# A conditioned transformer layer on one core: queue order of transfers, times of the norm's steps, and the place of one subtraction

## The chip, the cores and the metric

The kernel runs on one core of a Trainium2 chip. The core has five engines with a program each: TensorE (PE in the profile; its weight loads are PEld), VectorE (DVE), ScalarE (ACT), GpSimd (POOL) and SyncE (SP, which here issues nearly all DMA transfers). Every engine works through its own instructions in order and waits on semaphores for the others. The metric is the device time of one launch in microseconds (us); lower is better.

## The reference

One layer of a transformer with adaptive layer norm, over 8 sequences of 1024 tokens with 512 features, all in fp32:

```python
mod = silu(condition) @ Wada + bada
sh_a, sc_a, gt_a, sh_m, sc_m, gt_m = split(mod, 6)
xm = layernorm(x, g1, be1) * (1 + sc_a) + sh_a
x = x + gt_a * attention(xm, Wqkv, Wproj, bproj)   # causal, 16 heads of 32
xm = layernorm(x, g2, be2) * (1 + sc_m) + sh_m
x = x + gt_m * (gelu(xm @ W1 + b1) @ W2 + b2)      # 512 -> 2048 -> 512
```

## The kernel before

**Blocks.** The tokens are cut into 16 blocks n of 512 tokens; blocks 2b and 2b+1 are the halves of sequence b. A block goes through: load of x (`load_x`, tile hat), norm a, q, k and v, attention with its own keys and those of the earlier half, projection with the residual (`load_xr`, tile xr), norm m, four up steps with gelu (tiles hT), four down parts, and the store. The blocks are interleaved by a table, `plan` (L273 to L317): while the attention of block w runs, the projection and the feed-forward of block w-1 and the norm and q, k, v of the next blocks are put between its matmuls, so that TensorE has products to do while softmax work goes on elsewhere.

**Products.** Each 512-wide linear product is done by seven half-size products instead of eight (the Strassen-Winograd form, `strassen`, L959). Sums of weight quarters are made once and kept in DRAM (kept_qkv_S, kept_proj_S, kept_up_S, kept_down_S); sums of activations (t_a, t_m, t) are made per block. For the down product the halves of the gelu's output hT are the operands: B12 stands for the second token half, and the product needs B12 minus B11. `combine` (L1294, its operation at L1299) makes this difference in place on DVE at the start of down part 0. All linear matmuls go through `matmul` (L233) into one of three PSUM banks; results leave through `copy_out` (L214 or L217) and `combine_out` (L222).

**Attention.** For the row maxima, scores go to sc (L1692), DVE adds the mask (L1706) and reduces (L1709); the maxima are split in bf16 terms (mcols, L1728 to L1731), transposed by TensorE (L1747) and copied (mrow, L1753). Transposed scores st start with minus the maximum (L1773) and add the products (L1785); ACT takes the exponent into pT (L1798), POOL masks it (affine select, L1803) and adds the chunks of keys up (L1911), TensorE multiplies with v (po, L1826), and `finish` (L1836) sums over the keys by a product with ones (L1847). ACT inverts the sum (rec) and POOL or DVE scales.

**Weights and transfers.** Weight pieces of 256 KB come through a ring of nine tiles w. `fetch` (L380) issues a piece as soon as a ring tile is released; a piece is issued at L390, a kept sum at L392. SP issues in order, so a transfer that waits holds back those behind it. The other transfers are: loads of x for a norm (L432 and L438), loads of xr (L1443), stores of the output (L1276), gate rows, and the way by which a block is transposed for most norms. That way is `turn_rows` (L758): DVE turns squares of 32 by 32, four puts (L776, 256 KB each) write them to DRAM, and one get (L782, 1 MB) reads all channels back into xm; then DVE (L841) or ACT (L847) applies scale and shift to a channel group at a time.

**The planner.** The order on every engine is fixed while the program is built. The kernel keeps a clock for each engine (`now`), and for each piece of data the time when it will be written or left (`note`, `due`). Work that isn't due waits in lists: `jobs` for DVE (statistics, turns), `pool_jobs` for residual adds, `excursions` for ACT steps of a norm (root and apply, set off at fixed places of the attention by `run_excursions`), `transfers` for puts, gets and stores. Between matmuls `step_aside` (L1552) and `work` put out what has come due. `either` (L179) gives an elementwise operation to DVE (L187) or POOL (L190), whichever its clocks say ends first. `run_transfers` (L628 on) lets the earliest transfer out when its time has come and keeps 700 ns between two; the loads of x and xr don't pass through it and are issued where the plan has them. The planned time of a get is 7000 ns behind the last put, and its data count as there 5000 ns later; xr rows count as there 10000 ns after the load, and 700 ns more for each further tile. `finish` begins with `run_jobs(True)`, which puts out all waiting DVE jobs whether due or not. `settle` (L1258) multiplies a down result by its gate and adds it to xr, through `either`.

Of the kernel before, what the change touches and what calls it, by code (L numbers as in the profile page):

```python
# [22 lines left out]
def kernel(  # L23
# [261 lines left out]
    for w in range(1, NB):  # L285
        n = w - 1
        m = mlp_steps(n)
        even = blocks[n][1] == 0
        rows_a = [("rows", blocks[n][0], "a")] if even else []
        rows_m = [("rows", blocks[n][0], "m")] if even else []  # L290
        at = [("at", w + 2)] if w + 2 < NB else []
        ups = m[:1] + ([("load_xa", w + 2)] if w + 2 < NB else []) + m[1:3]
        ups += ([("norm_a", w + 2)] if w + 2 < NB else []) + m[3:4] + at
        head = rows_a + [("load_xr", n)]
        if w == 1:
            steps = head + [("k", w + 1), ("proj", n), ("mt", n), ("q", w + 1)]
# [12 lines left out]
        if w == NB - 1:  # L309
            plan[w] += late + downs[:2]  # L310
            downs = downs[2:]
# [113 lines left out]

    def load_x(n):
        b, h = blocks[n]
        rows = row_tile(f"hat_{n}")
        if is_turned(f"a{n}"):
            for a in range(P // SQ):  # L430
                r0 = h * TB + a * P
                nc.sync.dma_start(  # L432
                    rows[a * SQ : (a + 1) * SQ, :, :],
                    x[b, r0 : r0 + P, :].rearrange("(t r) d -> r t d", r=SQ),
                )
        else:
            for t in range(NTT):
                nc.sync.dma_start(rows[:, t, :], x[b, h * TB + t * P : h * TB + (t + 1) * P, :])  # L438
        return [rows[:, t, :] for t in range(NTT)]

    x_pre = {0: load_x(0)}
    ada = {}
# [184 lines left out]

    transfers = []  # L628
# [23 lines left out]
    def excursion(job, reads, first=False):  # L652
        if alone[0]:
            job()
        else:
            excursions.insert(0 if first else len(excursions), (job, reads))
# [16 lines left out]
    def normalize(tiles, key, sources):  # L673
# [7 lines left out]

        def statistics(t):
            st = small.tile([P, nc.vector.BN_STATS_DIM], F32, tag="st", name=f"st_{key}_{t}")
            nc.vector.bn_stats(st, tiles[t])
            nc.vector.bn_aggr(mv[:, t, :], st)
# [62 lines left out]
    def turn_first():  # L748
# [7 lines left out]
        first_turned.append(st)  # L756

    def turn_rows(key, tiles, xm):  # L758

# [3 lines left out]
        def turn(t):  # L763
            nc.vector.transpose(
                squares[:, :, ts(t, SQ)], tiles[t].rearrange("p (k r) -> p k r", r=SQ)
            )
            note("DVE", 700, [("hat", key, t)], [])
            if t == NTT - 1:
                ready = now["DVE"] + SYNC
                for a in range(P // SQ):  # L770
                    transfers.append((ready, lambda a=a: put(a)))

        def put(a):
            if a == P // SQ - 1:
                transfers.append((queue_free[0] + 7000, get))
            nc.sync.dma_start(  # L776
                there[:, ts(a, P)].rearrange("(k r) n -> r k n", r=SQ),
                squares[a * SQ : (a + 1) * SQ, :, :],
            )

        def get():
            nc.sync.dma_start(xm, there.rearrange("(c p) n -> p c n", p=P))  # L782
            written["spread", key] = queue_free[0] + 5000

        written["spread", key] = NEVER
        for t in range(NTT):
            add_job(lambda t=t: turn(t), [("hat", key, t)], key)

    def modulated(key, gain, shift, b, guards):
# [27 lines left out]
        if rows_turned:  # L817
            turn_rows(key, got, xm)
            yield [("spread", key)], []
        for c in range(NC):  # L820
            if rows_turned:
                if c:
                    yield [("spread", key)], []
                from_ps, held = xm[:, c, :], ("spread", key)
            elif turned is None:
# [271 lines left out]

    residual, stored, unstored = {}, {}, []
    y_count, y_keys = [0], {}

    def y_key(kind, new=False):
# [4 lines left out]
        return y_keys[kind]  # L1106
    LANDING = 10000

# [27 lines left out]
    def project_half(n):  # L1136
# [5 lines left out]
        for t in range(NTT):  # L1142
            xt_job = lambda t=t: add_to(
                residual[n][:, t, :], gate_rows["gba"], [("row", "gba")], [("xr", n, t)]
            )
            pool_jobs.append((xt_job, [("xr", n, t)]))

        def put(f, t, bank, ps, other, reads, last):
# [7 lines left out]
            else:  # L1156
                combine_out(y, bank, ps, other, reads, [ky], last=last)
                add_to(y, gate, [("row", "ga")], [ky], ALU.mult)
            add_to(residual[n][:, half(t, 2), c], y, [ky], [("xr", n, 2 * t), ("xr", n, 2 * t + 1)])

        def done():
            run_pool_jobs(True)
            normalize([residual[n][:, t, :] for t in range(NTT)], f"m{n}", [("xr", n, t) for t in range(NTT)])
# [5 lines left out]
    def project_out(n):  # L1169
# [4 lines left out]
        for t, xt in enumerate(tiles):  # L1174
            xt_job = lambda t=t, xt=xt: add_to(xt, gate_rows["gba"], [("row", "gba")], [("xr", n, t)])
            pool_jobs.append((xt_job, [("xr", n, t)]))
# [47 lines left out]
    def up(step):  # L1224
        _, n, q = step

        def gelu():
            for i in range(NC):
# [4 lines left out]
                k = q // 2 + 1  # L1233
                note_act(590, "gelu", [("h", n, q)], [(n, f"B{k}1"), (n, f"B{k}2"), ("g", n, q)])

        def finished():
# [4 lines left out]
        if (n, q) == (0, 0):  # L1241
            yield ["prepared up"], []
        written["g", n, q] = NEVER
        hT = act.tile([P, NC, TB], F32, tag="hT", name=f"hT_{n}_{q}", bufs=NQ)
        hTs[n, q] = hT
# [20 lines left out]
    def store(n, t):  # L1266
# [3 lines left out]
        stored[n + 1] = max(stored.get(n + 1, 0.0), ready)  # L1270
        unstored.append(n)

        def move():
            unstored.remove(n)
            for i in (2 * t, 2 * t + 1):
                nc.sync.dma_start(rows[i], residual[n][:, i, :])  # L1276

        transfers.append((ready + 1000, move))

# [4 lines left out]
    def down(n, part):  # L1284
# [133 lines left out]
    def perform(step):  # L1418
# [9 lines left out]
        elif kind == "load_xa":  # L1428
            x_pre[step[1]] = load_x(step[1])
            written["x", f"a{step[1]}"] = now["PE"] + 6000  # L1430
        elif kind == "load_xr":
# [7 lines left out]
            else:  # L1439
                xr = xrp.tile([P, NTT, D], F32, tag="xr", name=f"xr_{n}")  # L1440
            residual[n] = xr
            for t, rows in enumerate(row_tiles_of(x[b, h * TB : (h + 1) * TB, :], n)):
                nc.sync.dma_start(xr[:, t, :], rows)  # L1443
                landed = max(now["PE"], stored.get(n - 1, 0.0)) + LANDING + 700 * t
                written["xr", n, t] = landed
        elif kind == "norm_a":
# [72 lines left out]
    def work():  # L1519
# [11 lines left out]
        run_jobs()  # L1531
        run_pool_jobs()
        run_transfers()
        run_preparation()
# [17 lines left out]
    def step_aside(reads, writes):  # L1552
# [14 lines left out]
        run_jobs()  # L1567
        run_pool_jobs()
        run_transfers()
        run_preparation()  # L1570
# [525 lines left out]
```

## Time and profile before

| what | value |
|---|---|
| median of 3 runs | 3471.28 us (3470.78 to 3471.49) |
| the profiled execution | 3470.92 us |
| its span (first to last instruction) | 3469.2 us |
| granted TensorE clock, mean | 1.000 |
| DMA traffic | 489.91 MB, mean 141 GB/s |
| moved per issue, weights | 256 KB |
| LDWEIGHTS and matmul records | 55,442 each |

The page gives the busy time of each engine as a sum and a share of the span. The list of waits gives, for an engine and a line, what it waited for: the total in us, how often, and the longest. A timeline row gives the start, the duration from first to last of the grouped instructions, the engine, the line, the operation with output and input tiles, and in brackets the idle time of the engine just before, with what ended it. A window row gives for a stretch each engine's busy time with its count of instructions, then the granted clock of TensorE, the share of busy DMA engines and GB/s. Groups give count, then busy us and mean ns, then the idle time before them. The slices of the page show TensorE at 0.9 or more in all but the first of 40:

```profile
PE   8999999999999999999999999999999999999999
```

### The profile page before, as it was taken

How to read it: one execution, taken by the hardware profiler on the slowest of the kernel's cores; microseconds unless marked ns; L12 is line 12 of the kernel's file. 1: busy time of each engine (PE TensorE's matmuls, PEld its weight loads, DVE VectorE, ACT ScalarE, POOL GpSimd, SP SyncE). 2: the span in 40 equal slices, each digit the busy share in tenths (PEclk: the TensorE clock that was granted, in tenths of full speed). 3: DMA queues.
4: the chain of work that ended last, by engine and by line, in shares of the span. 5: the costliest groups of instructions: out<-in, count | busy, mean ns of one | idle time of the engine just before them, and what ended most of it. 6: DMA issues, size and time to landing. Idle time of an engine off the chain costs nothing.

```text
span 3469.2 us, 122474 instructions
## 1 busy us (share of the span) xinstructions
PE 3423.4 (99%) x55442; PEld 1778.0 (51%) x55442; DVE 2055.4 (59%) x2262; ACT 1301.4 (38%) x1444; POOL 1944.2 (56%) x2101
## 2 busy tenths in 40 slices
PE   8999999999999999999999999999999999999999
PEld 5544554555545554455554555454554545544555
DVE  6765666646565465664756547575466745656364
ACT  2345244343343433434333353443524334242421
POOL 3766757656267471774626755277553774446530
PEclk9999999999999999999999999999999999999999
DMA  6833434345544454444544445444464454633444
GB/s 226 277 127 87 120 108 138 109 117 159 156 141 134 127 152 146 138 136 128 167 135 144 136 132 175 127 140 135 133 187 121 129 150 121 187 115 88 120 143 136
DMA packets 378508, 489.91 MB, mean 141 GB/s; under 512 B 27284, under 2 KB 234444, under 8 KB 377988
## 3 DMA queue, kind: packets, MB, share of 16 engines
q1 hardware_dynamic: 377792, 481.79, 47.1%
q8 instruction: 437, 7.16, 0.9%
q14 instruction: 83, 0.68, 0.1%
q10 hardware_dynamic: 196, 0.28, 0.0%
HBM read 428.44 MB, written 53.53 MB: 139 GB/s over the span
## 4 chain that ended last, share of the span: by engine, by line
PE 89%; DVE 4%; DMA 4%; ACT 1%; issue 1%; POOL 1%; SPq 0%; DVEq 0%; ACTq 0%; POOLq 0%
PE bank L233 62%; PE sc L1692 8%; PE po L1826 7%; PE st L1785 7%; PE st L1773 3%; DVE mx L1709 2%; DMA w<-kept_proj_S 2%; PE bank L1847 2%; DMA w<-in_L_cond_Wproj_dram 1%; DVE sc L1706 1%; ACT pT L1798 1%; DMA xm_m<-turned_m 1%; PE bank L1747 0%; DVE hT L1299 0%; DMA xr<-in_x_dram 0%
## 5 line engine op out<-in xcount | busy, mean ns | idle before, releaser
L1911 POOL TENSOR_TENSOR pT<-pT,pT 128x256 f32<-128x256 f32 (+3 forms) x1254 | 1213.5, 1003 | 143.1 <-ACT pT L1798 112.3
L1798 ACT ACTIVATE pT<-st 128x2048 f32<-128x2048 f32 x288 | 541.1, 1879 | 1075.2 <-PE st L1785 989.3
L233 PE MATMUL bank<-w,hT 128*32 128x256 f32 x14336 | 814.1, 380 | 0.0
L1709 DVE TENSOR_REDUCE mx<-sc 128x4 f32<-128x2048 f32 (+3 forms) x384 | 665.7, 1754 | 215.3 <-PE sc L1692 209.2
L233 PEld LDWEIGHTS bank<-w,hT 128*32 128x32 f32 x14336 | 454.5, 110 | 357.6 <-issue 74.7
L233 PE MATMUL bank<-xm_m,w 128*32 128x256 f32 x8192 | 500.7, 381 | 4.6 <-DVE xm_m L841 4.5
L1803 POOL TENSOR_SCALAR_AFFINE_SELECT pT<-pT 128x512 f32<-128x512 f32 x256 | 177.1, 710 | 436.8 <-ACT pT L1798 431.5
L233 PE MATMUL bank<-t_m,w 128*32 128x256 f32 x6144 | 384.2, 381 | 0.1
L233 PEld LDWEIGHTS bank<-xm_m,w 128*32 128x32 f32 x8192 | 257.2, 110 | 228.7 <-issue 65.1
L1692 PE MATMUL sc<-kT,qT 32*128 32x512 f32 (+3 forms) x3072 | 329.3, 520 | 2.9 <-DVE mx L1709 1.8
L1706 DVE TENSOR_TENSOR sc<-sc,mask 128x1024 f32<-128x1024 f32 (+1 forms) x160 | 162.8, 1017 | 242.9 <-PE sc L1692 167.2
L1826 PE MATMUL po<-pT,v 128*32 128x512 f32 (+3 forms) x3072 | 304.9, 491 | 0.0
L1785 PE MATMUL st<-qT,kT 32*128 32x512 f32 (+3 forms) x3072 | 300.1, 486 | 0.0
L233 PEld LDWEIGHTS bank<-t_m,w 128*32 128x32 f32 x6144 | 190.2, 110 | 178.4 <-issue 51.7
L233 PE MATMUL bank<-xm_a,w 128*32 128x256 f32 x3968 | 239.3, 380 | 2.4 <-ACT xm_a L847 1.1
L190 POOL TENSOR_TENSOR qT<-top,rec 128x512 f32<-128x512 f32 x60 | 78.5, 1309 | 276.1 <-ACT rec L1865 276.1
L222 DVE TENSOR_TENSOR hT<-bank,u_u 128x512 f32<-128x512 f32 x192 | 130.0, 686 | 153.2 <-PE bank L233 150.7
L1692 PEld LDWEIGHTS sc<-kT,qT 32*128 32x128 f32 x3072 | 129.7, 184 | 161.5 <-issue 54.7
L233 PE MATMUL bank<-w,qT 128*32 128x256 f32 (+1 forms) x2944 | 191.6, 399 | 3.2 <-DMA w<-in_L_cond_Wproj_dram 3.2
L233 PE MATMUL bank<-t_a,w 128*32 128x256 f32 x2944 | 181.7, 380 | 0.0
L233 PEld LDWEIGHTS bank<-xm_a,w 128*32 128x32 f32 x3968 | 127.7, 110 | 97.4 <-issue 13.9
L1230 ACT ACTIVATE hT<-hT,cols 128x512 f32<-128x512 f32 x256 | 164.2, 711 | 27.2 <-DVE hT L222 26.5
(240 smaller groups left out, 3418.2 us busy)
## 6 DMA issues: line engine op xcount, KB each, us to landing
w<-in_L_cond_W_dram SPq DMA_DIRECT2D x384, 256.0 KB
w<-kept_up_S SPq DMA_DIRECT2D x256, 256.0 KB
w<-kept_down_S SPq DMA_DIRECT2D x256, 256.0 KB
w<-kept_qkv_S SPq DMA_DIRECT2D x180, 256.0 KB
w<-in_L_cond_Wqkv_dram SPq DMA_DIRECT2D x147, 256.0 KB
hat<-in_x_dram SPq DMA_DIRECT2D x64, 256.0 KB
xr<-in_x_dram SPq DMA_DIRECT2D x64, 256.0 KB
out_dram<-xr SPq DMA_DIRECT2D x64, 256.0 KB
```

The lines of the kernel that those rows point to most:

```text
L222: nc.vector.tensor_tensor(out, src, other, op)
L233: nc.tensor.matmul(ps[r], columns, rhs, start=start, stop=stop, skip_group_check=True)
L1230: nc.scalar.activation(hT[:, i, :], hT[:, i, :], AF.Gelu, bias=cols[:, O_B1 + f : O_B1 + f + 1])
L1692: nc.tensor.matmul(sc[:, j, c0 : c0 + w], qTs[n][r, gg, ts(qt, P)], keys_of(n, kh)[r, gg, :w], start=True, stop=True, skip_group_check=True,)
L1706: nc.vector.tensor_tensor(place, place, shape_of.to_broadcast(place.shape), ALU.add)
L1709: nc.vector.tensor_reduce(maxima[n, gg][:, kh, qt, :], sc[:, :, c0 : c0 + w], axis=AX.X, op=ALU.max)
L1773: nc.tensor.matmul(st[:, j, c0 : c0 + w], minus_ones[r, :], row[r, TB - w :], start=(c0 == 0), stop=False, skip_group_check=True,)
L1785: nc.tensor.matmul(st[:, j, c0 : c0 + w], kT[r, gg, ts(k % NTT, P)], qT[r, gg, TB - w :], start=False, stop=True, skip_group_check=True,)
L1798: nc.scalar.activation(pT[:, :, :used], st[:, :, :used], AF.Exp, scale=scale)
L1803: nc.gpsimd.affine_select(diagonal, diagonal, pattern=[[0, HPG], [1, P]], compare_op=ALU.is_ge, fill=0.0, base=0, channel_multiplier=-1,)
L1826: nc.tensor.matmul(po[r, TB - w :], v[:, k % NTT, g * P + j * hd : g * P + (j + 1) * hd], pT[:, j, c0 : c0 + w], start=(k == 0), stop=last ...
L1911: nc.gpsimd.tensor_tensor(into, into, pT[:, j, c0 : c0 + w], ALU.add)
```

## The change

1. Transfers get a rank: puts and gets first, then loads of x and xr, then stores. `run_transfers` takes the lowest rank among those that are due and keeps 1700 ns between two instead of 700. The loads of x and xr now pass through this queue too; a consumer calls `arrived`, which puts the queue out where the load hasn't been issued yet. A store of two tiles becomes two transfers. The planned landing of an xr row becomes 6000 ns after its issue.
2. The get becomes four, one for each channel group of 256 KB, planned 5500 ns behind the last put and counted as there 3000 ns after the issue; scale and shift of a group wait for its own part.
3. Root and apply of a norm are put out by `run_ready` as soon as they are due, if ACT holds the table for the exponent. The gelus, which enter the same list with `first`, keep their set places.
4. The difference B12 minus B11 becomes a DVE job added behind the gelu of up steps 0 and 1; down part 0 waits for it ahead of its second product.
5. From the second sequence on, the gate rows of the attention are loaded one window earlier.

```diff
-        rows_a = [("rows", blocks[n][0], "a")] if even else []
+        rows_a = [("rows", blocks[n][0], "a")] if n == 0 else []
...
-        plan[w] = steps + rows_m + ups[:i]
+        rows_a = [("rows", blocks[w][0], "a")] if not even else []
+        plan[w] = steps + rows_m + rows_a + ups[:i]
...
+        for to, from_x in pairs:
+            later(lambda to=to, from_x=from_x: nc.sync.dma_start(to, from_x))
...
+    PATH, LOAD, STORE = range(3)
+    SPACE = 1700
...
-            i = min(range(len(transfers)), key=lambda i: transfers[i][0])
-            if not everything and max(queue_free[0], transfers[i][0]) > now["PE"]:
+            due_now = [i for i, (ready, *_) in enumerate(transfers) if ready <= now["PE"]]
+            if everything:
+                i = min(range(len(transfers)), key=lambda i: transfers[i][0])
+            elif queue_free[0] > now["PE"] or not due_now:
                 return
-            ready, transfer = transfers.pop(i)
-            queue_free[0] = max(queue_free[0], now["PE"], ready) + 700
+            else:
+                i = min(due_now, key=lambda i: transfers[i][1::-1])
+            ready, _, transfer = transfers.pop(i)
+            queue_free[0] = max(queue_free[0], now["PE"], ready) + SPACE
...
+    def run_ready():
+        while excursions and excursions[0][2]:
+            if table[0] != "exp" or max(now["ACT"], due(excursions[0][1])) > now["PE"]:
+                return
+            excursions.pop(0)[0]()
...
-                transfers.append((queue_free[0] + 7000, get))
+                for c in range(NC):
+                    transfers.append((queue_free[0] + LANDED, PATH, lambda c=c: get(c)))
...
-        def get():
-            nc.sync.dma_start(xm, there.rearrange("(c p) n -> p c n", p=P))
-            written["spread", key] = queue_free[0] + 5000
+        def get(c):
+            nc.sync.dma_start(xm[:, c, :], there[ts(c, P), :])
+            written["spread", key, c] = queue_free[0] + 3000
...
+    def arrived(what):
+        while what in coming:
+            run_transfers(True)
...
-    LANDING = 10000
+    LANDING = 6000
...
+            if q < NQ // 2:
+                add_job(difference, [("g", n, q)], ("difference", n))
+
+        def difference():
+            b12, b11 = hT[:, :, HB:], hT[:, :, :HB]
+            nc.vector.tensor_tensor(b12, b12, b11, ALU.subtract)
...
-            for i in (2 * t, 2 * t + 1):
-                nc.sync.dma_start(rows[i], residual[n][:, i, :])
-        transfers.append((ready + 1000, move))
+        for i in (2 * t, 2 * t + 1):
+            unstored.append(n)
+            transfers.append((ready + 1000, STORE, lambda i=i: move(i)))
...
-            combine(nc.vector, "B12", "B12", "B11")
             bank, ps = yield from product("B11")
...
+            yield [("difference", n, q) for q in range(NQ // 2)], []
             bank, ps = yield from product("B12")
...
+                coming.append(("xr", n))
+                transfers.append((now["PE"], LOAD, lambda t=t, rows=rows: load(t, rows)))
...
         run_jobs()
         run_pool_jobs()
+        run_ready()
         run_transfers()
```

More of the change, by code (lines that the diff above doesn't have):

```diff
@@ L424, in row_tile, with load_x @@
         return tmp.tile([P, NTT, D], F32, tag="hat", name=name, bufs=1)
-    def load_x(n):
+    def load_x(n, later):
         b, h = blocks[n]
         rows = row_tile(f"hat_{n}")
+        pairs = []
         if is_turned(f"a{n}"):
@@ L655, in excursion @@
         else:
-            excursions.insert(0 if first else len(excursions), (job, reads))
+            excursions.insert(0 if first else len(excursions), (job, reads, not first))
     def run_excursions(limit=None):
@@ L682, in statistics @@
         def statistics(t):
+            arrived(("x", key))
             st = small.tile([P, nc.vector.BN_STATS_DIM], F32, tag="st", name=f"st_{key}_{t}")
@@ L779, in put @@
             )
-        def get():
-            nc.sync.dma_start(xm, there.rearrange("(c p) n -> p c n", p=P))
-            written["spread", key] = queue_free[0] + 5000
-        written["spread", key] = NEVER
+        def get(c):
+            nc.sync.dma_start(xm[:, c, :], there[ts(c, P), :])
+            written["spread", key, c] = queue_free[0] + 3000
+        for c in range(NC):
+            written["spread", key, c] = NEVER
         for t in range(NTT):
@@ L818, in modulated @@
             turn_rows(key, got, xm)
-            yield [("spread", key)], []
+            yield [("spread", key, 0)], []
         for c in range(NC):
@@ L822, in modulated @@
                 if c:
-                    yield [("spread", key)], []
-                from_ps, held = xm[:, c, :], ("spread", key)
+                    yield [("spread", key, c)], []
+                from_ps, held = xm[:, c, :], ("spread", key, c)
             elif turned is None:
@@ L1174, in project_out @@
         for t, xt in enumerate(tiles):
-            xt_job = lambda t=t, xt=xt: add_to(xt, gate_rows["gba"], [("row", "gba")], [("xr", n, t)])
+            xt_job = lambda t=t, xt=xt: arrived(("xr", n)) or add_to(xt, gate_rows["gba"], [("row", "gba")], [("xr", n, t)])
             pool_jobs.append((xt_job, [("xr", n, t)]))
@@ L1234, in gelu @@
                 note_act(590, "gelu", [("h", n, q)], [(n, f"B{k}1"), (n, f"B{k}2"), ("g", n, q)])
+            if q < NQ // 2:
[3 more added lines that the diff above has]
+            nc.vector.tensor_tensor(b12, b12, b11, ALU.subtract)
+            keys = [(n, "B11"), (n, "B12"), ("g", n, q)]
+            note("DVE", 1250, keys, [(n, "B12"), ("difference", n, q)], port=True)
         def finished():
@@ L1243, in up @@
         written["g", n, q] = NEVER
+        written["difference", n, q] = NEVER
         hT = act.tile([P, NC, TB], F32, tag="hT", name=f"hT_{n}_{q}", bufs=NQ)
@@ L1270, in store, with move @@
         stored[n + 1] = max(stored.get(n + 1, 0.0), ready)
-        unstored.append(n)
-        def move():
+        def move(i):
             unstored.remove(n)
-            for i in (2 * t, 2 * t + 1):
-                nc.sync.dma_start(rows[i], residual[n][:, i, :])
-        transfers.append((ready + 1000, move))
+            nc.sync.dma_start(rows[i], residual[n][:, i, :])
+        for i in (2 * t, 2 * t + 1):
+            unstored.append(n)
+            transfers.append((ready + 1000, STORE, lambda i=i: move(i)))
     def stored_by(n):
@@ L1428, in perform, with later, landing @@
         elif kind == "load_xa":
-            x_pre[step[1]] = load_x(step[1])
-            written["x", f"a{step[1]}"] = now["PE"] + 6000
+            key = ("x", f"a{step[1]}")
+            def later(load):
+                coming.append(key)
+                transfers.append((now["PE"], LOAD, lambda: landing(load)))
+            def landing(load):
+                load()
+                coming.remove(key)
+                written[key] = NEVER if key in coming else queue_free[0] + 4000
+            written[key] = NEVER
+            x_pre[step[1]] = load_x(step[1], later)
         elif kind == "load_xr":
@@ L1441, in perform, with load @@
             residual[n] = xr
+            def load(t, rows):
+                coming.remove(("xr", n))
+                nc.sync.dma_start(xr[:, t, :], rows)
+                written["xr", n, t] = max(now["PE"], stored.get(n - 1, 0.0), queue_free[0]) + LANDING
             for t, rows in enumerate(row_tiles_of(x[b, h * TB : (h + 1) * TB, :], n)):
-                nc.sync.dma_start(xr[:, t, :], rows)
-                landed = max(now["PE"], stored.get(n - 1, 0.0)) + LANDING + 700 * t
-                written["xr", n, t] = landed
+                written["xr", n, t] = NEVER
+                coming.append(("xr", n))
+                transfers.append((now["PE"], LOAD, lambda t=t, rows=rows: load(t, rows)))
         elif kind == "norm_a":
@@ L1568, in step_aside @@
         run_pool_jobs()
+        run_ready()
         run_transfers()
```

20 lines of the change are left out of this document (11 added, 9 removed).

## The prediction

> **What bounds the kernel now.** I read the page first, then the waits of TensorE, then the timeline round each long wait, and last the order of the two built programs.
>
> ```profile
> PE 3423.4 (99%) x55442; PEld 1778.0 (51%) x55442; DVE 2055.4 (59%) x2262; ACT 1301.4 (38%) x1444; POOL 1944.2 (56%) x2101
> ```
>
> ```profile
> PE st L1773 <- DVE mx L1709: 7.5, 12, 1.9
> PE bank L1747 <- POOL mcols L1731: 5.9, 7, 1.6
> ...
> PE bank L233 <- DVE xm_m L841: 4.5, 1, 4.5
> ...
> PE bank L233 <- DMA w<-in_L_cond_Wproj_dram: 3.2, 2, 1.6
> PE bank L233 <- DMA w<-kept_proj_S: 2.3, 4, 0.8
> ...
> PE sc L1692 <- DVE mx L1709: 1.8, 5, 0.6
> ...
> PE bank L832 <- ACT xm_m L847: 0.4, 1, 0.4
> PE bank L832 <- ACT xh_m L709: 0.4, 1, 0.4
> ```
>
> TensorE is busy 3423.4 of 3469.2 us; 45.8 us are idle. The compiled order of both programs holds the same 29,078 matmul instructions, and the count of changes of tile shape goes from 1187 to 1186, so the busy time stays. The change can only take waits away or add them, and what it can take is bounded by 45.8 us.
>
> **What the change removes.** *The long wait for a get.* In the timeline (start, duration, engine, line):
>
> ```profile
> 1300.26 1.97 SPq L1276 DMA_DIRECT2D out_dram<-xr  x2
> ...
> 1310.71 1.18 SPq L782 DMA_DIRECT2D xm_m<-turned_m  x1
> ...
> 1321.78 1.01 DVE L841 TENSOR_SCALAR xm_m<-xm_m,gainm,shiftm 128x512 f32<-128x512 f32 x2 [8.19 <-DMA xm_m<-turned_m]
> ...
> 1322.43 3.51 PE L233 MATMUL bank<-xm_m,w 128*32 128x256 f32 x32 [4.48 <-DVE xm_m L841]
> ...
> 1326.15 1.93 PE L233 MATMUL bank<-xm_a,w 128*32 128x256 f32 x32 [0.21 <-DVE u_k L222]
> ```
>
> ```profile
> 1322.40:1326.00 3.60, 3.51 (x32) 1.69 (x32) 3.43 (x6) 0.21 (x2) 1.16 (x1) 0.53 0.16 57
> ```
>
> The 1 MB get left at 1310.71, behind stores, and its reader started 11.07 us later. TensorE lost 4.48 us; then 32 matmuls took 3.51 us instead of the 1.93 us of the next 32, and the window row gives a granted clock of 0.53 there: 1.58 us more. With the 0.21 behind it: 6.3. In the new order the last quarter of this get leaves some 27 us of matmuls ahead of its use (before, 1322.43 - 4.48 - 1310.71 = 7.2), and stores rank last. Gone: 6.3. The Trainium skill, "TensorE: Matmul & The Clock Gate", section "What's actually happening", says that the array falls to half clock after an idle window of about 3.4 us and needs as long at work to come back; the row agrees, and by that rule each new wait of this length costs its own length and some 1.6 us more.
>
> *Projection weights behind the residual's rows.*
>
> ```profile
> 777.30 2.46 SPq L1443 DMA_DIRECT2D xr<-in_x_dram  x4
> ...
> 783.57 1.29 POOL L190 TENSOR_TENSOR xr<-xr,row_gba 128x512 f32<-128x512 f32 x1 [12.47 <-DMA xr<-in_x_dram]
> ...
> 787.14 1.28 POOL L190 TENSOR_TENSOR xr<-xr,row_gba 128x512 f32<-128x512 f32 x1 [2.29 <-DMA xr<-in_x_dram]
> ...
> 790.99 1.26 POOL L190 TENSOR_TENSOR xr<-xr,row_gba 128x512 f32<-128x512 f32 x1 [2.57 <-DMA xr<-in_x_dram]
> ...
> 794.50 1.94 PE L233 MATMUL bank<-w,t 128*32 128x256 f32 x32 [0.82 <-DMA w<-kept_proj_S]
> ```
>
> Four 256 KB loads issued together land 6.3, 9.8 and 13.7 us after the first (their readers wait for nothing else), so 3.6 to 3.9 us apiece; the pieces of Wproj issued behind them come 0.82 late. The two rows of waits for Wproj and kept_proj sum to 5.5 us in six places. In the new order the four loads are 7 us of matmuls apart and one of them, not four, stands ahead of the first kept_proj piece. Gone: 5.5. If the spaced loads still fill the same path, only half goes: 2.7.
>
> *Start of the first m norm.* The two L832 rows (0.8) go: the norm's root and apply run when due. Gone: 0.8. Sum 12.6.
>
> **What it adds.** *End of the second block's attention.*
>
> ```profile
> 374.05 0.40 PE L1773 MATMUL st<-mrow,minus_ones 32*128 32x512 bf16 x4
> ...
> 375.46 1.88 ACT L1798 ACTIVATE pT<-st 128x2048 f32<-128x2048 f32 x1 [10.58 <-PE st L1785]
> ...
> 378.53 1.28 POOL L190 TENSOR_TENSOR xr<-xr,v_d 128x512 f32<-128x512 f32 x1
> 379.76 0.63 POOL L1803 TENSOR_SCALAR_AFFINE_SELECT pT<-pT 128x512 f32<-128x512 f32 x1
> 380.48 5.88 POOL L1911 TENSOR_TENSOR pT<-pT,pT 128x512 f32<-128x512 f32 x4
> ...
> 382.59 0.94 DVE L187 TENSOR_TENSOR p_d<-p_d,u_d 128x512 f32<-128x512 f32 x1
> ...
> 383.66 6.68 PE L233 MATMUL bank<-w,hT 128*32 128x256 f32 x120
> ...
> 385.25 1.65 DVE L187 TENSOR_TENSOR xr<-xr,p_d 128x512 f32<-128x512 f32 x1
> ...
> 386.31 1.67 POOL L1803 TENSOR_SCALAR_AFFINE_SELECT pT<-pT 128x512 f32<-128x512 f32 x2
> ...
> 387.95 5.54 POOL L1911 TENSOR_TENSOR pT<-pT,pT 128x384 f32<-128x384 f32 x8
> ...
> 392.77 1.82 PE L1847 MATMUL bank<-pT,ones 128*32 128x512 f32 x8
> ```
>
> Before, 18.72 us lie between the first scores of the last two key chunks (374.05) and the closing sum (392.77), and POOL's selects and adds for them run from 379.76 to 393.49: they end as TensorE needs them. In the new order two things differ. 60 instructions (120 records, the 6.68 us of one row) of the down product no longer stand between these points: 12.04 us are left. And the three operations at L187 on p_d (first and last shown), which `either` gave to DVE, are given to POOL ahead of the selects: 3 x 1.28 = 3.84. So, from the first scores: exp ends at 3.29; POOL begins with p_d by about 2.9 and ends it at 6.7; its chunk work then takes 13.7 as measured beside DVE, or 12.9 with adds of 1.28: it ends at 19.6 to 20.4 against 12.04. The last four adds can overlap the first matmuls of the sum, about 0.7. New wait: 6.9 to 7.7, taken 7.2. No product is left that TensorE could do there: all of that block's down parts and qkv stand before, the next ones behind. With 1.6 for the clock as at 1322: 8.8. If POOL's adds shrink to their fastest and p_d starts earlier, 5; if contention stretches them, 10.
>
> *End of the eighth block's attention.*
>
> ```profile
> 1614.83 0.68 DVE L684 BATCH_NORM_STATS2 st_a<-hat 128x6 f32<-128x512 f32 x1
> 1615.15 2.56 ACT L1230 ACTIVATE hT<-hT,cols 128x512 f32<-128x512 f32 x4
> ...
> 1617.93 0.18 DVE L685 BATCH_NORM_AGGREGATE mv_a<-st_a 128x2 f32<-128x6 f32 x1
> 1618.04 1.21 DVE L1706 TENSOR_TENSOR sc<-sc,mask 128x1024 f32<-128x1024 f32 x1
> 1619.28 2.35 DVE L1709 TENSOR_REDUCE mx<-sc 128x4 f32<-128x1536 f32 x2
> ...
> 1622.15 0.40 PE L1773 MATMUL st<-mrow,minus_ones 32*128 32x384 bf16 x8
> ```
>
> ```profile
> L1299 DVE TENSOR_TENSOR hT<-hT x32: 1207/2292/2311, 306.9 to 3418.6; 128x1024 f32<-128x1024 f32 x32
> ```
>
> `finish` flushes all waiting DVE jobs. In the new order the difference stands first among them, and it needs this gelu, which ends at 1617.71; the four statistics, which ran during the gelu before (3.28 us from 1614.83 to 1618.11), stand behind it, then mask and reduce. 1617.71 + 0.1 + 1.21 to 2.29 + 3.28 + 1.21 + 2.35 = 1625.9 to 1626.9 against 1622.15, which is 11.6 us of matmuls behind the preceding scores in both orders. New wait 3.7 to 4.8, taken 3.8; whether the clock falls here is open (0 to 1.6, taken 0).
>
> *The rest.* Waits of 0.4 to 1.9 us for the row maxima (7.5 + 5.9 + 1.8 = 15.2 in 24 places) come from what happens to stand ahead on DVE and POOL; the new order takes some away and makes others of 0.6 to 1.1. I take their sum as unchanged, give or take 4.
>
> **Edits costed at nothing.** The hat loads now pass through the queue by rank: DVE waited 0.2 us for them in all, and they still leave some 30 us ahead. Splitting each get adds three issues (1.18 us for the one at 1310.71) on SP; SP is in order and weights wait behind, but its own waits are for ring tiles that TensorE still holds, so the time is there:
>
> ```profile
> L684 DVE BATCH_NORM_STATS2 st_a<-hat 128x6 f32<-128x512 f32 x64 | 42.9, 670 | 0.2 <-DMA hat<-in_x_dram 0.2
> ```
>
> ```profile
> SPq L392 <- PE bank L233: 1436.5, 682, 21.8
> ```
>
> If four quarters follow each other as the four xr loads did (6.3 + 3 x 3.7 = 17.4), the get of the eighth block's a norm, whose last quarter has 10.8 us of matmuls ahead, would be 6.6 late; its rows are whole 2 KB lines on all partitions, so I take 0. The Trainium skill speaks against the split: "DMA: Bandwidth & Descriptors", section "Anatomy of one DMA — SWDGE (gpsimd) path", gives about 2 us fixed per DMA on another queue kind, 6 us more per get if they ran in series; no run here shows that for gets. Thirty scale-and-shift operations go from ACT to DVE, which idles 41%. Of the 64 differences at L1299, 32 move behind the gelu; TensorE's list of waits names none at L1299. Gate rows a window earlier: a load with nothing behind it that TensorE waits for.
>
> **Sum.** -12.6 + 8.8 + 3.8 = 0.0 against the profiled execution (3470.92: span 3469.2 and 1.72 around it); the median of the runs is 0.36 above that. Forecast 3471.
>
> **Rivals.**
> A, faster: the repeating small waits shrink. DVE no longer does the difference between two products, the root stands earlier, so maxima come sooner; if half of the 15.2 us go, 3471 - 7.6 = 3463. For: 12 of the waits end on DVE's reduce. Against: the differences now stand near the gelu, beside the attention's own reduces. With the first added wait at its low end (-4), 3460.
> B, slower: the moved difference collides with the maxima as at the eighth block. At 1622 DVE had 0.5 us to spare (reduce ends 1621.63); a difference of 1.21 to 2.29 ahead of a reduce costs 0.7 to 1.8 wherever it lands within that lead. At 10 of 32 places it gives 7 to 18, so 3478 to 3489, taken 3482; it decides once more than six places collide. For: the job list is flushed at every `finish`. Against: in the order I find one clear collision and three below 1.2.
> C: the change doesn't do what it says, gets and projection weights stay late (spaced loads still queue), while the added waits come: 0.5 x 12.6 back, 3477, or all, 3484.
>
> **How the numbers follow.** Runs of this kernel differ by 0.7 us; 0.2% (6.9 us) is taken as the bound of no change. Forecast, within 3464.3 to 3478: 0.52; A 0.21; B 0.16; C 0.11, a part of it inside the bound (0.03). Faster 0.21, same 0.55, slower 0.24. The range, 3461 to 3482, takes most of A and the low half of B and C.
>
> **What would show it.** Right: no wait for xm_m over 1 us and no wait for Wproj or kept_proj in TensorE's list; a wait of 5 to 9 us for POOL's pT adds at the closing sum near 391 us with the clock at about a half behind it; one of about 4 us for mx near 1624; TensorE's busy time within 4 us of 3423. Wrong: POOL done with the adds by then, more than three new waits of over 1 us for mx, or waits for xm_a on a late quarter.

## The result and the profile after

| kernel | median us | ratio to before, 95% interval |
|---|---|---|
| before | 3471.11 (22 runs) | 1 |
| changed | 3466.64 (22 runs, 3463.39 to 3467.89) | 0.9986 (0.9980 to 0.9992) |

The change takes 0.14% (4.9 us by the ratio, with an interval of 2.8 to 6.9) away. That is a gain beyond the noise of so many runs, and within the 0.2% that the prediction took as no change; the forecast of 3471 was 4.4 us above. The profiled execution took 3464.49 us with a span of 3462.7, 6.4 us under that of before.

The page's first part, of the changed kernel; TensorE's busy time is that of before within 0.1 us, so by these two sums the difference lies in its waits (the busy time includes what half clock adds):

```profile
PE 3423.5 (99%) x55442; PEld 1774.7 (51%) x55442; DVE 2079.4 (60%) x2313; ACT 1289.2 (37%) x1424; POOL 1924.6 (56%) x2070
```

TensorE's waits in the changed kernel (sum, count, longest):

```profile
PE st L1829 <- DVE mx L1765: 13.1, 7, 4.4
...
PE bank L1803 <- POOL mcols L1787: 2.2, 2, 1.6
...
PE bank L1903 <- POOL pT L1967: 1.0, 1, 1.0
PE bank L233 <- DVE p_proj L214: 0.9, 2, 0.6
PE bank L1803 <- DVE mcols L1787: 0.9, 1, 0.9
...
PE sc L1748 <- DVE mx L1765: 0.3, 1, 0.3
```

What is no longer in the list agrees: no wait for xm_m by DVE (it was 4.5) and none for a piece of Wproj or kept_proj (they were 5.5). The waits that end on the row maxima were 15.2 in 24 places before (7.5, 5.9 and 1.8); now they are 13.1 + 2.2 + 0.9 + 0.3 = 16.5 in 11 places, and two long ones hold 7.9 of it. The other nine come to 8.6.

The two long ones stand where the prediction put two new waits. End of the second block, in the timeline of the changed kernel:

```profile
377.73 0.39 PE L1829 MATMUL st<-mrow,minus_ones 32*128 32x512 bf16 x4
...
381.52 1.27 POOL L190 TENSOR_TENSOR p_d<-p_d,u_d 128x512 f32<-128x512 f32 x1 [0.96 <-DVE u_d L222]
...
387.14 1.14 PE L1748 MATMUL sc<-kT,qT 32*128 32x512 f32 x8
388.03 1.64 DVE L187 TENSOR_TENSOR xr<-xr,y_d 128x512 f32<-128x512 f32 x1
389.59 0.69 DVE L1762 TENSOR_TENSOR sc<-sc,mask 128x512 f32<-128x512 f32 x1
390.31 2.29 DVE L1765 TENSOR_REDUCE mx<-sc 128x4 f32<-128x2048 f32 x1
...
392.66 0.40 PE L1829 MATMUL st<-mrow,minus_ones 32*128 32x512 bf16 x4 [4.38 <-DVE mx L1765]
392.88 1.68 PE L1841 MATMUL st<-qT,kT 32*128 32x512 f32 x8
393.15 5.49 POOL L1967 TENSOR_TENSOR pT<-pT,pT 128x384 f32<-128x384 f32 x8
394.50 1.94 PE L1882 MATMUL po<-pT,v 128*32 128x384 f32 x16
397.47 2.28 PE L1903 MATMUL bank<-pT,ones 128*32 128x512 f32 x8 [1.04 <-POOL pT L1967]
```

The closing sum starts 19.74 us after the first scores of the last chunks (377.73); by the prediction's measure the matmuls between them are 12.04 long, so 7.7 us are lost: 5.7 are waits (4.38, 1.04 and one of 0.24), 1.5 is the clock, and 0.5 is not assigned. TensorE lost most of it ahead of the sum: scores for the maxima end at 388.28, DVE is at the last down part's residual add until 389.67, then masks and reduces, and the next scores wait 4.38. What follows runs at half clock (1.68 us where 1.03 stood before, 1.94 where 1.07), and only then does the sum wait 1.04 for POOL, whose adds end at 398.64.

End of the eighth block:

```profile
1613.19 1.23 DVE L1268 TENSOR_TENSOR hT<-hT 128x1024 f32<-128x1024 f32 x1 [2.83 <-ACT hT L1258]
1614.34 0.69 DVE L701 BATCH_NORM_STATS2 st_a<-hat 128x6 f32<-128x512 f32 x1
...
1617.55 1.21 DVE L1762 TENSOR_TENSOR sc<-sc,mask 128x1024 f32<-128x1024 f32 x1
...
1621.20 0.40 PE L1829 MATMUL st<-mrow,minus_ones 32*128 32x384 bf16 x8 [3.53 <-DVE mx L1765]
1621.43 1.55 PE L1841 MATMUL st<-qT,kT 32*128 32x384 f32 x16
1622.91 3.10 PE L233 MATMUL bank<-t_m,w 128*32 128x256 f32 x32
```

Difference, four statistics, mask and reduce stand in a row on DVE, as read from the order. The wait is 3.53, and the matmuls behind it take 1.55 where 1.09 stood before and 3.10 where 1.91 did: 1.65 more, 5.2 in all.

### The profile page after: what moved, and what is told of

It reads as the page before. It is cut to its first block, busy times and chain, and to the rows that moved or that the text cites. A ratio compares the mean times of both kernels' runs of the same rounds, so it can differ in the third digit from the quotient of the medians.

```text
span 3462.7 us, 122558 instructions
## 1 busy us (share of the span) xinstructions
PE 3423.5 (99%) x55442; PEld 1774.7 (51%) x55442; DVE 2079.4 (60%) x2313; ACT 1289.2 (37%) x1424; POOL 1924.6 (56%) x2070
## 4 chain that ended last, share of the span: by engine, by line
PE 92%; ACT 3%; DVE 2%; POOL 1%; issue 1%; DMA 0%; SPq 0%; ACTq 0%; DVEq 0%; POOLq 0%
PE bank L233 65%; PE sc L1748 8%; PE po L1882 7%; PE st L1841 7%; PE st L1829 3%; PE bank L1903 2%; ACT pT L1854 1%; ACT hT L1258 1%; DVE mx L1765 1%; POOL pT L1967 1%; PE bank L1803 0%; ACT L1258 0%; PE bank L853 0%; ACT L170 0%; DVE sc L1762 0%
## 5 line engine op out<-in xcount | busy, mean ns | idle before, releaser
L190 POOL TENSOR_TENSOR qT<-top,rec 128x512 f32<-128x512 f32 x50 | 65.5, 1311 | 246.1 <-ACT rec L1921 242.4
```

## The experiments

All ratios are to the kernel before on the same chip, with 95% intervals. The first seven variants take parts away from the change or add one or two to the kernel before; the others act on the queue and on the two new waits.

**no_split: the get in one transfer again.**

```diff
-                for c in range(NC):
-                    transfers.append((queue_free[0] + LANDED, PATH, lambda c=c: get(c)))
+                transfers.append((queue_free[0] + 7000, PATH, get))
...
+            nc.sync.dma_start(xm, there.rearrange("(c p) n -> p c n", p=P))
```

> The changed kernel with the get in one 1 MB transfer again (planned 7 us behind the last put, counted as there 5 us later); all else as changed. Places theory (the time is the sum of the waits that TensorE shows, each with a cause of its own, and the get at 1310 us was late because of its place in the queue): the same as the changed kernel within 2 us, about 3466, no wait for xm_m over 1 us. Rival (the split itself cured the late get): the 4.5 us wait with its half clock is back, 3472.

Measured: 3466.52 us, 0.9985 (0.9976 to 0.9994), no wait for xm_m over 0.4 us. The split has no measurable effect here; it did not cure the late get.

**no_ready: root and apply at their set places.**

```diff
-        while excursions and excursions[0][2]:
+        while False and excursions[0][2]:
```

> The changed kernel with the norm's root and apply left at their set places. Places theory: the waits for xh_m and xm_m at the first m norm come back (0.8), and the m norm of the sixth block is turned later, so that part of its late get comes back (2 to 5): 3468 to 3472. Rival (early root and apply hide nothing): 3466 to 3467, no wait for xm_m.

Measured: 3469.25 us, 0.9997 (0.9987 to 1.0006). The two waits of 0.4 at the first m norm are back, and near 1328 us TensorE waits 1.64 and 0.37 at the first use of the sixth block's xm_m, then 2.02 for a reduce behind its scale and shift. The places theory holds; the part is worth some 3 us beside the others, though the interval overlaps that of the changed kernel.

**no_diff: the difference back in down part 0.**

```diff
-            if q < NQ // 2:
-                add_job(difference, [("g", n, q)], ("difference", n))
...
+            combine(nc.vector, "B12", "B12", "B11")
             bank, ps = yield from product("B11")
...
-            yield [("difference", n, q) for q in range(NQ // 2)], []
```

> The changed kernel with the difference for the down product back at the start of down part 0. Places theory: the wait of 3.6 us at the end of the eighth block's attention and its half clock go (-5), but about 7 waits of about 1 us for the difference itself and as many for the row maxima behind it come (+10 to +15): 3471 to 3477. Rival (the moved difference only made the collision at the eighth block): 3461.

Measured: 3483.42 us, 1.0035 (1.0023 to 1.0048), above what was expected. TensorE's waits in this kernel:

```profile
PE st L1827 <- DVE mx L1763: 15.8, 14, 4.6
PE bank L233 <- DVE hT L1334: 12.5, 6, 2.1
```

The difference now makes TensorE wait six times for about 2.1 us, which it did not do once in the kernel before. In the timeline the first of these:

```profile
595.56 2.36 DVE L187 TENSOR_TENSOR xr<-xr,row_gba 128x512 f32<-128x512 f32 x2
...
597.84 2.35 DVE L1334 TENSOR_TENSOR hT<-hT 128x1024 f32<-128x1024 f32 x2
599.11 1.27 PE L233 MATMUL bank<-w,hT 128*32 128x256 f32 x17 [2.08 <-DVE hT L1334]
```

In this order the residual adds of xr stand right ahead of the difference on DVE. Behind four of the six waits the clock is halved for 3.41 us as well. So beside the other parts, moving the difference is worth some 17 us. That it only made the collision at the eighth block is refuted.

**queue_only: the transfers' part and the gate rows alone.**

The three edits above together, on the changed kernel.

> The kernel before with the ranks, the spacing, the loads through the queue and the gate rows moved, but the get in one, root and apply at their set places and the difference in down part 0. Places theory: TensorE's waits for Wproj and kept_proj go (-5.5), the late get of the sixth block stays (3 to 6), no new wait at the ends of the second and eighth blocks: 3465 to 3467. Rival (the gain of the whole change is the norm's and the difference's doing, spaced loads change nothing): 3470 to 3472 with the projection waits there.

Measured: 3472.64 us, 1.0004 (0.9995 to 1.0013), above the expected range; neither theory fits as stated. The waits:

```profile
PE st L1827 <- DVE mx L1763: 13.8, 15, 2.2
PE bank L1801 <- POOL mcols L1785: 5.9, 7, 1.6
...
PE bank L233 <- ACT xm_m L868: 2.8, 1, 2.8
PE bank L233 <- DVE hT L1334: 2.8, 1, 2.8
```

The waits for Wproj and kept_proj are gone, as the places theory said; of the late get 2.8 are left. But the maxima wait 21 us in all where it was 15, and the difference 2.8. What the spaced loads win, the longer small waits and a half clock behind each of the two waits of 2.8 take back.

**ready_only, diff_only, ready_diff: the other parts on the kernel before.** `run_ready` as in the change, called behind `run_pool_jobs` at both places; the difference as in the change; both.

> The kernel before with root and apply of a norm as soon as due, nothing else. Places theory: the wait at the first m norm (0.8) goes, the late get of the sixth block goes because its norm is turned earlier (-6), the end of the second block brings the 4.4 us wait for the maxima and its half clock (+6), projection waits stay; some 10 places where the difference or the projection's sums now come in the way of TensorE (+5 to +15): 3472 to 3485. Rival (early root alone pulls the maxima forward): 3463 to 3467.

Measured: 3473.41 us, 1.0007 (0.9997 to 1.0017), inside the range of the places theory. The late get is gone, the waits for maxima are there (20.7 in 23, one of them 4.58 at the end of the second block), and new ones for the projection's sums (u_proj, 3.4 in 6).

> The kernel before with the difference made behind the gelu, nothing else. Places theory: the waits at the ends of the second and eighth blocks come (+7 and +5), the late get and the projection waits stay: 3478 to 3484. Rival (moving the difference is what made the maxima come sooner): 3462 to 3468.

Measured: 3512.68 us, 1.0114 (1.0100 to 1.0128), far above.

> The kernel before with both the early root and apply and the difference behind the gelu, no change of the transfers. If the transfers' part is what makes the other two pay: late gets and projection waits at several blocks stay, the ends of the second and eighth blocks cost 12: 3480 to 3500. If the two parts are sound by themselves: 3464 to 3472 (the changed kernel's 3466.6 plus 0 to 5.5 of projection waits).

Measured: 3497.65 us, 1.0073 (1.0052 to 1.0093), inside the first range. In both kernels one event returns three times. In ready_diff, near 1756 us:

```profile
1732.63 1.42 SPq L1291 DMA_DIRECT2D out_dram<-xr  x2
...
1736.07 2.27 SPq L1291 DMA_DIRECT2D out_dram<-xr  x2
...
1741.12 1.92 SPq L788 DMA_DIRECT2D xm_m<-turned_m  x1
...
1753.24 2.22 ACT L853 ACTIVATE xm_m<-xm_m,shiftm,gainm 128x512 f32<-128x512 f32 x3 [8.36 <-DMA w<-kept_up_S]
...
1755.37 0.56 ACT L217 COPY kT<-bank 128x512 f32<-128x512 f32 x1
...
1755.98 1.51 PE L233 MATMUL bank<-xm_m,w 128*32 128x256 f32 x12 [4.85 <-ACT kT L217]
```

It is the event of 1310 us in the kernel before: four stores, then a 1 MB get whose reader starts 12.1 us later. (The row names kT: the copy of kT out of its bank stands behind the scale and shift on ACT, and TensorE starts 0.05 us after it ends. The bracket at ACT names kept_up_S; in the trace the get had landed 0.1 us before it.) TensorE's list of waits has it three times in ready_diff, and in diff_only as often, beside the sixth block's (xm_m, 5.4):

```profile
PE bank L233 <- ACT kT L217: 15.2, 3, 5.5
```

```profile
PE bank L233 <- ACT kT L217: 15.6, 3, 5.5
```

The first fence is of ready_diff, the second of diff_only. Each such wait has a half clock with it, of 3.41 us in ready_diff and of 6.83 in diff_only, so it costs more than its length. In diff_only this is not all of the surplus: near 1883 us TensorE waits 4.66 behind a product of DVE that took 5.60 us, where the 13 on this row take 1.29 in the mean, and that wait too has 6.83 us of half clock.

```profile
1877.26 5.60 DVE L187 TENSOR_TENSOR qT<-t,qT 128x512 f32<-128x512 f32 x1 [4.16 <-POOL pT L1920]
```

Why the moved difference, without the spacing, brings the stores ahead of these gets is not shown. ready_only, whose transfers are spaced no further, has none of these waits.

**no_rank and space700: which part of the queue does it.**

```diff
-    PATH, LOAD, STORE = range(3)
+    PATH, LOAD, STORE = 0, 0, 0
...
-                i = min(due_now, key=lambda i: transfers[i][1::-1])
+                i = min(due_now, key=lambda i: transfers[i][0])
```

> The changed kernel with all transfers of one rank (the earliest due goes first); spacing 1700 as changed. If the rank keeps stores out of the gets' way: the late get of the sixth block returns in part, 3469 to 3473. If spacing and planned times do it and the rank decides almost nothing: the same as the changed kernel, 3465 to 3468, no wait for xm_m over 1 us.

Measured: 3465.86 us, 0.9983 (0.9974 to 0.9992). In the trace every engine has the changed kernel's instructions in the changed kernel's order: the rank never decides anything here.

```diff
-    SPACE = 1700
+    SPACE = 700
```

> The changed kernel with 700 ns between two transfers, as before, instead of 1700; ranks and the path through the queue stay. If the spacing matters (loads that move at 3.6 us apiece pile up and hold gets, rows and weights): waits for gets or for POOL behind xr rows at several blocks, 3475 to 3500. Rival (rank and queue do it, the spacing is free): 3465 to 3468.

Measured: 3503.24 us, 1.0090 (1.0075 to 1.0105). One constant is worth 37 us here. The profiled executions are 34.8 us apart (3499.26 and 3464.49): 21.5 of them are waits of TensorE, the rest is in its busy time, which includes two more half clocks of 3.41 us. Two rows of the waits:

```profile
PE bank L233 <- DVE u_k L222: 10.9, 6, 3.0
...
PE bank L233 <- DVE qT L222: 4.9, 3, 2.1
```

In the timeline of this kernel the quarters of a get leave between stores, and DVE, which has scale and shift in its order, stands at them:

```profile
1753.66 0.55 SPq L1311 DMA_DIRECT2D out_dram<-xr  x1
1754.29 0.43 SPq L802 DMA_DIRECT2D xm_m<-turned_m  x1
...
1761.50 0.55 DVE L862 TENSOR_SCALAR xm_m<-xm_m,gainm,shiftm 128x512 f32<-128x512 f32 x1 [2.73 <-DMA xm_m<-turned_m]
...
1763.41 0.68 DVE L222 TENSOR_TENSOR u_k<-bank,u_k 128x512 f32<-128x512 f32 x1
1764.15 1.93 PE L233 MATMUL bank<-xm_a,w 128*32 128x256 f32 x32 [2.96 <-DVE u_k L222]
```

A 256 KB quarter, planned to land in 3 us, has its reader 7.2 us later behind a store; DVE waits in its order, and TensorE waits for the sum u_k behind it.

**no_flush: the closing of a group puts out due jobs only.**

```diff
-        run_jobs(True)
+        while (i := next_job(now["PE"] + 500)) is not None:
+            jobs.pop(i)[0]()
```

> The changed kernel, where the closing of an attention group puts out only the DVE jobs that are due within 0.5 us, not all waiting ones. Places theory: at the end of the eighth block the difference and the statistics no longer stand ahead of mask and reduce; the wait of 3.5 us and 1.7 us of half clock behind it go: 3461.5 (-5). Rival (what is not flushed there collides a little later): 3465 to 3467, with new waits of 1 us or more elsewhere.

Measured: 3457.09 us, 0.9962 (0.9949 to 0.9974). The wait at the eighth block is gone with its half clock (5.2), and so are one of 1.7 us near 3130 and one of 0.7 near 1193: 7.6 in all. The gain over the changed kernel is 8 to 10 between the ratios and the medians, more than the 5 expected; the two other waits are 2.4 of the surplus. Between the profiled executions it is only 5.1: that of no_flush is the slowest of its five, 2.3 above their median, and that of the changed kernel is 2.2 below its own.

**p_dve and p_pool: the first block's gate products on one engine.** In `settle`, on top of no_flush (p_pool; p_dve has -1e9):

```diff
+        old, margin[0] = margin[0], 1e9 if n == 0 else margin[0]
         add_to(y, gate, [("row", "gm")], [ky], ALU.mult)
         add_to(residual[n][:, half(t, 2), c], y, [ky], keys)
+        margin[0] = old
```

> As no_flush, and the same operations all on DVE. If POOL's adds set the end of the second block: its wait goes, 3457.5. If DVE's order does: DVE has the first p_d operations earlier, where it idles, and the last part's as before, so the wait for the maxima stays at 1 to 4.4 us and the time between 3459 and 3462.

Measured: 3457.8 us, 0.9960 (0.9946 to 0.9973), the time of the first reading; the wait for the maxima is 1.35, as the second had it.

> As no_flush, and all gate products and residual adds of the first block's down parts on POOL. If DVE's order (the last part's gate and add ahead of mask and reduce) makes the 4.4 us wait for the row maxima at the end of the second block: it falls under 1 us, the closing sum waits 1 to 3 us for POOL, the clock holds; 4 us less than no_flush, 3457.5. If POOL's adds set the end there, as the prediction had it: POOL now has three operations more ahead (3.8 us), the wait of the closing sum grows to 5 to 9 us and the time to 3463 to 3466.

Measured: 3454.06 us, 0.9951 (0.9937 to 0.9964), the lowest median of all: 17 us under the kernel before, though the interval overlaps that of no_flush. At the end of the second block of p_pool:

```profile
384.01 1.14 PE L1750 MATMUL sc<-kT,qT 32*128 32x512 f32 x8
385.08 2.36 PE L233 MATMUL bank<-w,hT 128*32 128x256 f32 x40
...
388.37 0.40 PE L1831 MATMUL st<-mrow,minus_ones 32*128 32x512 bf16 x4 [0.92 <-DVE mx L1767]
...
393.24 2.29 PE L1906 MATMUL bank<-pT,ones 128*32 128x512 f32 x8 [2.62 <-POOL pT L1970]
```

What the reading by DVE's order named came (under 1 us, 1 to 3 us, the clock whole), but both chains had a share. With DVE's gate and add out of the way, and 40 records of the down product between scores and their use again, the wait for the maxima falls from 4.38 to 0.92; POOL's adds then cost 2.62, less than the 5 to 9 of the POOL reading. In p_dve the two are 1.35 and 3.28. In both kernels the planner also moved products, so how much is DVE's order and how much the products is not told apart.

## Why the prediction came out as it did

- **The late get.** Predicted gone, 6.3: gone. But the reason given in part, that stores rank last, is wrong: no_rank has the same order. Nor is it the split (no_split). ready_only has no such wait either, queue_only still has 2.8 and no_ready 1.64 and 0.37: the early root and apply account for most of it. As forecast, the last quarter left early: at 1301.42, some 26 us ahead of its first use at 1327.8 (forecast 27). ready_diff and space700 show that later blocks get the same wait, or one like it, where the difference is moved and the transfers are not spaced.
- **The projection weights.** Predicted -5.5: no DMA wait is left; 0.9 for a copy (p_proj) stands in its place. queue_only has none of these waits either, so the transfers' part does it. The spacing is not needed for it: space700 has none, though near 784 us its four loads of xr leave within 3.5 us. In both orders, as forecast, one load and not four stands ahead of the first kept_proj piece.
- **The first m norm.** Predicted -0.8; half came back as a wait for scale and shift (0.4).
- **End of the second block.** Predicted 8.8 with the clock, and the closing sum 19.2 us after the first scores; it came 19.74 after them, 7.7 lost. The size held, the name did not: instead of the 5 to 9 us named for POOL's adds TensorE waited 1.04 for them. The step "it ends at 19.6 to 20.4 against 12.04" was nearly right about POOL (its adds ended 20.9 after the first scores) but saw one of two late chains. DVE's chain ended earlier in the order and took 4.38 of the loss first. A chain that is late at the last consumer is not yet the one that TensorE stands at.
- **End of the eighth block.** Predicted 3.8, and the clock "taken 0": 3.53 and 1.65. no_flush takes both away.
- **The small waits.** "I take their sum as unchanged, give or take 4" is the term that was mis-sized: 15.2 became 8.6 beside the two long ones, -6.6. That is rival A's size nearly in full (it had -7.6), and it is what put the time 4.4 us under the forecast. The variants show which part does it. Without the long waits at the ends of the second and eighth blocks, the waits for the maxima come to 15.2 before, 16.1 in ready_only, 17.2 in no_diff and 20.9 in queue_only, where the difference stands in down part 0, and to 7.3 (ready_diff), 8.6 (changed), 8.8 (no_rank), 8.9 (space700), 9.1 (no_split), 10.6 (diff_only) and 11.6 (no_ready), where it is moved. So moving the difference shortens them in each of these orders, and the early root takes another 3 beside it.
- **The sum.** -6.3 - 4.6 - 0.4 + 7.7 + 5.2 - 6.6 = -5.0, against -6.4 between the two profiled executions. Of the 1.4 left, 0.9 lie at the start: the first long wait for the maxima (1.6) ends at 64.23 before and at 63.30 here, and between 62.52 and 65.30 in the other kernels, even 0.55 earlier in no_rank, which has the same program. The other 0.5 is not assigned. That the terms apart from the small waits came out at +1.6, where 0.0 was forecast, is in part luck: the second block was 1.1 too dear and the eighth 1.4 too cheap.
- **Rival B** did not come in the changed kernel (one collision of the difference, not ten). **Rival C's** half, gets and weights that stay late, came in ready_diff and diff_only, with the difference moved and without the spacing.
- **"Edits costed at nothing."** Here the argument was weaker than its result. TensorE's list named no wait for the difference, so moving it was costed at nothing; beside the other parts it is worth 17 us, and alone it costs about 40. The cover that hid it was an order on DVE that the other parts of the change rearrange. Likewise each single part is neutral or worse (1.0004, 1.0007, 1.0114), two of them 1.0073 (root and difference), 1.0035 (transfers and root, with the split) or 0.9997 (transfers and difference, with the split); a gain beyond the interval comes only with the three together.

## What to carry to other kernels

In a program whose order a planner fixes, the parts of a change are not terms of a sum: read the whole new order, and test each part with the others present and absent, before one is called useless or good. A wait list that doesn't name an operation says that it is hidden in this order, not that it is off the path in the next one. Where a list of jobs is flushed "whether due or not" ahead of something that TensorE will need, put out only what is due; and try a wider spacing of transfers: 1.7 us against 0.7 was worth 37 us here, where loads issued together landed 3.6 to 3.9 us apart (no other spacing was tried).

## What the runs showed of the hardware that was not expected

The length of a wait alone does not settle whether TensorE's clock falls. Of the six waits of 2.1 us in no_diff four halved it and two did not; one of 3.53 in the changed kernel halved it, and one of 3.52 in space700 (it ends at 1627.27) left it whole. What the traces show is a grid: a stretch of half clock lasts 3.41 us, or two or three times as long (6.83 in diff_only, 10.24 in no_flush), and the 1225.4 us between the two in the changed kernel are 359 pieces of 3.413. Laid on this grid, from 40 us on in all 14 kernels, the pieces just ahead of a fall have TensorE busy for at most 45% of their length, and of those that no half clock follows none has it busy for less than 40%. Window rows of pieces of the grid, TensorE's busy time being the second number and the granted clock the third from the end; the first two are of no_diff (its wait of 2.08 ends at 1027.33), the others of space700:

```profile
1024.14:1027.55 3.41, 1.32 (x28) 0.55 (x20) 3.41 (x4) 0.00 (x0) 1.45 (x1) 1.00 0.53 157
1027.55:1030.96 3.41, 3.41 (x36) 1.74 (x32) 3.41 (x3) 0.00 (x0) 0.00 (x0) 0.50 0.00 0
```

```profile
1622.21:1625.63 3.42, 1.54 (x32) 0.65 (x20) 3.32 (x6) 0.98 (x3) 1.29 (x1) 1.00 0.57 147
1625.63:1629.04 3.41, 1.77 (x36) 1.17 (x40) 2.85 (x5) 0.31 (x1) 1.01 (x4) 1.00 0.11 41
```

The wait of no_diff lies in one piece, the longer one of space700 is shared by two. So a wait of 2 to 3.5 us costs some 1.6 us more, or nothing, by where it falls; every wait of 4.38 us and more had a half clock with it, from 40 us on. The Trainium skill, "TensorE: Matmul & The Clock Gate", section "What's actually happening", puts the idle window at about 3.4 us. The length of the pieces agrees with that, but here a piece in which TensorE was busy for 1.32 us of 3.41 was followed by half clock, so it need not be idle throughout.

The difference itself took less time where it stands behind the gelu, 1302 ns in the mean against 1931. Groups of lines, mean ns of one behind the comma, of the kernel before and of the changed one:

```profile
L1299 DVE TENSOR_TENSOR hT<-hT 128x1024 f32<-128x1024 f32 x32 | 60.6, 1931 | 0.0
```

```profile
L1268 DVE TENSOR_TENSOR hT<-hT 128x1024 f32<-128x1024 f32 x32 | 41.7, 1302 | 16.3 <-ACT hT L1258 16.3
```
